# A post-LN attention and LoRA-FFN layer: the first two units' queries by seven products, the keys by tiles, gathers and sums in other slots, the end in another order

## The chip, the cores and the metric

The kernel runs on one NeuronCore of a Trainium2 chip. The metric is the time of one execution on the device in microseconds; a profiled execution gives the span from the first to the last instruction and the trace. The engines are TensorE (PE in the profile; its weight loads are PEld), VectorE (DVE), ScalarE (ACT), GpSimd (POOL) and SyncE (SP, which issues most of the DMAs here).

## The reference

The input x is 2 batches of 512 tokens of width 512, all in float32.

```python
q = x @ Wq + bq                  # 32 heads of 128
k = x @ Wk + bk ; v = x @ Wv + bv # 8 groups of 128
q, k = rope(q), rope(k)
scores = causal(q @ k.T / sqrt(128))     # each group serves 4 heads
ctx = softmax(scores) @ v
x = layernorm(x + ctx @ Wo + bo)

y = x @ W_base.T + b_base
z = x @ lora_A[active].T                 # 4 experts of rank 8
alpha = softmax(log(prior[active] + eps) + x @ router_W.T + router_b)
x = layernorm(x + y + sum_e alpha_e * 2 * z_e @ lora_B[e].T)
```

## The kernel before

**Units and slots.** A unit is a pair of a group (4 heads) and a batch; there are 16. After a setup written out by hand, the program is a sequence of slots T from -8 on; `slot(T)` issues what each engine does in that slot, and `put(T, f)` adds a step at its end. Each unit has 16 slots of attention: the slot's scores are one product of 128 rows (4 heads x 32 tokens) by up to 512 keys (`score`, L552), then VectorE's masked maximum (L560), ScalarE's exponential (L567), one slot apart each, with two banks of PSUM for scores. The order on every engine is the order of the program: it is a manual schedule, and each engine takes its instructions in that order.

**Products.** From unit 2 on, the queries of two heads and the output projection of two tiles are made by Strassen's scheme: seven products of half size in place of eight. `q_products(u, k, step)` (L440 by way of `product`) makes product `step` for the pair of heads k of unit u, in two half banks qx and qy. It needs sums of the weights (`w_sums`, four POOL instructions, L427 to L430), of which product 5 uses the first, 6 the second, 3 the third and 7 the fourth, and sums of x (`x_sums`, four VectorE instructions, L419). Products 1, 2 and 4 use weights as they are loaded. ScalarE copies a result out of qx (`q_copy`, L476) and VectorE adds qy (`q_sum`, L480). Rope takes three VectorE instructions a head (L374, L377, L381) and one POOL sum (L382). `wo_sums` (L637) are four VectorE sums of the output weights of a group, ahead of its products (`wo_products`).

**Setup before the change.** SP loads the four x tiles of the first batch, Wk of group 0, Wq of group 0, rope, Wq's second half, Wv, the second batch of x. POOL fills constants and two large zero tiles, issues six small DMAs of the expert indices (L217 to L220), an iota and two memsets (L227). TensorE turns the four x tiles (L281), multiplies the keys of unit 0 in four products of 512 columns (`k_mm`, L361), then unit 0's queries in sixteen plain products (`q_mm`, L361) with value tiles (`v_tile`, L344) and the second batch's transposes between. Unit 1's queries, sixteen plain products too, go one to each slot from -8 to 7. The prior's row (`prior_weights`) is three steps in slots -4 to -2; six gathers (`gather_experts`, indirect DMAs that POOL issues, L265) stand in slot -8; two steps of `lora_weights` in slots 12 and 16; sums of x of batch 0 in slots 0 to 3, of batch 1 in 12 to 15; `x + bo` (POOL, L899) in slots 2 to 9.

**The end.** From slot 237 on, the FFN of the first batch (f0) is mixed into the last units: W_base is loaded and turned (`transposed_base`), its copies on ScalarE. After the last slot, a hand-written order follows for the remaining tiles: fz (last of the first batch), fa (two), fb, fc. Each is `base` (x by W_base, L778), `logits` and `alphas` (VectorE, and an exponential on ScalarE), `low_rank` (a transpose, L814, and a copy, L815), `finish` (L819), `sum` (L829), statistics (L703), root (L711, ScalarE; inverse on VectorE) and `store`. `add` is `sum` and statistics.

Of the kernel before, what the change touches and what calls it, by code (L numbers as in the profile page):

```python
# [15 lines left out]
P = 128  # L16
# [13 lines left out]
def postln_layer_kernel(  # L30
# [117 lines left out]

    def load_k(g):
        wk_g = wts.tile([P, KC, D], F32, tag="wk_g", name=f"wk_{g}")  # L150
        nc.sync.dma_start(out=wk_g, in_=Wk[:, ts(g, D)].rearrange("(c p) n -> p c n", p=P))
        wqk["k", g] = wk_g
# [34 lines left out]
    nc.gpsimd.memset(eps_sb, LN_EPS)  # L187
    nc.gpsimd.memset(bmT, 0.0)
    for z in zt:
        nc.gpsimd.memset(z, 0.0)  # L190

    bqk = setup.tile([NBIAS, D], F32, name="bqk")
    nc.scalar.dma_start(out=bqk[:H, :], in_=bq.rearrange("(h d) -> h d", d=D))
    nc.scalar.dma_start(out=bqk[H : H + G, :], in_=bk.rearrange("(h d) -> h d", d=D))
    nc.scalar.dma_start(out=bqk[H + G :, :], in_=bv.rearrange("(h d) -> h d", d=D))
    for t in range(TPB):
        load_x(t, 1)
    load_k(0)
    load_q(0, 0)
# [69 lines left out]

    def gather_experts():  # L270
        gather(ar_act[:EAR, :], lora_A.rearrange("e r n -> (e r) n"), idx["a"])
        gather(ar_act[EAR : EAR + EA, :], router_W, idx["e"])
        for a in range(EA):
            gather(b_act[:, a, :], lora_B.rearrange("e (p j) r -> (e p) (j r)", j=BJ), idx["b"][:, a : a + 1])


    def transpose_token_tile(dst, src, pool, tag, copy):

        tp = pool.tile([P, KC, P], F32, tag=tag, name="tp")
        for c in range(KC):  # L280
            nc.tensor.transpose(tp[:, c, :], src[:, ts(c, P)], ident)  # L281
        copy(dst, tp)

    b_jar = setup.tile([P, BJ, EA, RK], F32, name="b_jar")

    def lora_weights(step):
        if step == 0:
            ta = ps_wo.tile([P, KC, EAR + EA], F32, tag="wx", name="ta")
            for c in range(KC):
                nc.tensor.matmul(  # L290
                    ta[:, c, :], lhsT=ar_act[:, ts(c, P)], rhs=ident[:, : EAR + EA], start=True, stop=True)
            nc.vector.tensor_copy(arT, ta)
            nc.vector.tensor_copy(b_jar, b_act.rearrange("p a (j r) -> p j a r", r=RK))
        else:

            tbm = ps_wo.tile([EAR, BJ, P], F32, tag="wx", name="tbm")
# [6 lines left out]
    def prior_weights(step):  # L303

        if step == 0:
            pr_eps = setup.tile([EA, 1], F32, name="pr_eps")
            nc.vector.tensor_scalar(pr_eps, pr_act, PRIOR_EPS, None, ALU.add)
            pr["lp"] = setup.tile([EA, 1], F32, name="lp")
            nc.scalar.activation(pr["lp"], pr_eps, AF.Ln)
        elif step == 1:  # L310
            lpb = setup.tile([EA, 1], F32, name="lpb")
            nc.vector.tensor_tensor(lpb, pr["lp"], rb_act, ALU.add)
            ones = setup.tile([EA, P], F32, name="ones")
            nc.vector.memset(ones, 1.0)
            nc.vector.tensor_scalar(lp_rep[:EA, :], ones, lpb, None, ALU.mult)
        else:
            pl = ps_wo.tile([P, EA], F32, tag="wx", name="pl")
            nc.tensor.matmul(pl, lhsT=lp_rep, rhs=ident[:, :EA], start=True, stop=True)
            nc.vector.tensor_copy(lp_bc, pl)
# [65 lines left out]
    def k_mm(u, c):  # L385
        g, b = unit(u)
        proj_mm(("k", u), ps_k, "k", wqk["k", g], slice(0, D), b, c)

    def k_of(u):
        if u not in kT:  # L390
            kT[u] = work.tile([P, UNIT, BLK], F32, tag="kT", name=f"kT_{u}", bufs=5)
        return kT[u]

    def k_rope(u, part):
        if part == 0:
            k_of(u)
        rope_step(("k", u), H + unit(u)[0], part, kT[u])

    def q_mm(u, r, c, pool, tag):

        g, b = unit(u)
        proj_mm(("q", u, r), pool, tag, wqk["q", set_of(u), r // 2], ts(r % 2, D), b, c)

# [10 lines left out]

    def x_sums(b, step):
# [3 lines left out]
        nc.vector.tensor_tensor(  # L419
            *((t1, b12, b11), (t2, b22, t1), (t3, b22, b12), (t4, b21, t2))[step], ALU.subtract)  # L420
# [541 lines left out]
    def slot(T):  # L962

        uq, step = divmod(T + 24, UNIT)
        kq, step = divmod(step, 8)
        now = B <= uq < NU
        if now and step != 7 and step != 4:
            q_products(uq, kq, {0: 2, 1: 6, 2: 5, 3: 7, 5: 4, 6: 3}[step])
        un, kn = (uq, 1) if kq == 0 else (uq + 1, 0)
        if B <= un < NU and step == 7:  # L970
            q_products(un, kn, 1)
        plain_q = T - T_BEGIN < UNIT and divmod(T - T_BEGIN, QB)
        if plain_q:
            r, c = plain_q
            q_mm(1, r, c, *q_banks[r])
        uk, l = divmod(T + UNIT, UNIT)
# [52 lines left out]
        kr, sr = divmod(sr, 8)  # L1029
        if B <= ur < NU and sr < 6:  # L1030
            q_rope(ur, 2 * kr + (sr < 3), sr % 3)
        r, part = divmod(T - T_BEGIN - QB, QB)
        if 0 <= r < R and part < 3:
            q_rope(1, r, part)
        k_slots = (4, 5, 6) if uk < PLAIN_K else (11, 13, 14) if uk < NU - 1 else (3, 5, 6)
# [9 lines left out]
    spare = ((ps_wo, "wx"), (ps_wo, "wy"), (ps_ctx, "ctx"), (ps_sc, "sc"))  # L1045
    q_banks = ((ps_q, "qx"), (ps_q, "qy"), (ps_q, "qx"), (ps_wo, "wy"))
# [6 lines left out]
    tb = ps_sc.tile([P, NBIAS], F32, tag="sc", name="tb")  # L1053
    nc.tensor.transpose(tb, bqk, ident[:NBIAS, :NBIAS])
    nc.vector.tensor_copy(bqkT, tb)
    for c in range(KC):
        k_mm(0, c)
    for part in range(3):
        k_rope(0, part)
    expert_rows()  # L1060

    for r in range(R):
        for c in range(KC):
            q_mm(0, r, c, *q_banks[r])
        for part in range(3):
            q_rope(0, r, part)
        if r == 2:
            for t in range(TPB, NT):
                transpose_token_tile(xT[:, :, ts(t, P)], x_sb[:, t, :], *spare[t % 2 + 2], nc.scalar.copy)
        elif r:  # L1070
            v_tile(0, r // 2, *spare[r // 2 * 2])
            v_out(0, r // 2)
    for t in range(2, TPB):
        v_tile(0, t, *spare[t % 2 * 2])
        v_out(0, t)

# [79 lines left out]
    f0[2].norm2.stats(2, f0[2].y)  # L1156
    f0[0].norm2.root(0, 3)
    for f in f0[:3]:
        f.store()
# [5 lines left out]
    fb.transpose(*CTX)  # L1165
    fz.logits()
    fz.alphas()
    for r in range(R):
# [105 lines left out]
```

## Time and profile before

| What | Value |
|---|---|
| runs | 822.33, 823.33, 825.24 us; median 823.33 |
| the profiled execution | 822.99 us |
| its span | 821.2 us |
| TensorE | busy 810.6 us, granted clock 0.999 |
| VectorE, ScalarE, POOL | busy 603.7, 379.2, 320.9 us |
| DMA | 116.00 MB, mean 141 GB/s |
| first product of the keys; of unit 0's queries | at 8.38; at 11.92 us |
| first product of a slot's scores | at 45.62 us |
| last product | starts at 815.2 us |

Times in rows of the trace are from the start of the span. A row of the timeline gives start, duration, engine, line, operation, the tensors written and read, and the shape; "x8" is eight merged records. A float32 matmul shows as two records. Busy time of an engine is not by itself time that can be saved: what matters is what ends the wait of the engine that sets the end.

### The profile page before, as it was taken

The numbers are of one execution on the slowest core, as the hardware profiler recorded it, in microseconds if no ns is written. First come the engines' busy times: TensorE is split into PE (matmuls) and PEld (weight loads), VectorE is DVE, ScalarE is ACT, GpSimd is POOL, SyncE is SP. The second block draws the span as 40 slices with busy tenths as digits, with TensorE's granted clock in tenths as the row PEclk, the third lists the DMA queues.
The fourth block names the chain that finished last, engine by engine and source line by source line (L and its number), as shares of the span: only waits on it lengthen the run. The fifth ranks groups of instructions, "written<-read, shape, count | busy, mean of one in ns | idle before, by whom it ended". The sixth has DMA issues, their size and how long they took to land.

```text
span 821.2 us, 11196 instructions
## 1 busy us (share of the span) xinstructions
PE 810.6 (99%) x3385; PEld 598.5 (73%) x3385; DVE 603.7 (74%) x1972; ACT 379.2 (46%) x1058; POOL 320.9 (39%) x377
## 2 busy tenths in 40 slices
PE   8999999999999999999999999999999999999996
PEld 5567777777777778777777878777777878655565
DVE  4367877677878876787868777787888689974455
ACT  1236453453545554444545444444545454663244
POOL 6464343512543545321453245343464333420033
PEclk9999999999999999999999999999999999999999
DMA  9015636445474637354454627355453726674211
GB/s 306 22 39 148 213 77 174 134 118 163 103 208 107 201 91 218 90 141 156 135 150 126 190 66 224 97 154 180 134 148 96 225 65 183 187 257 142 77 39 65
DMA packets 84415, 116.00 MB, mean 141 GB/s; under 512 B 6525, under 2 KB 64237, under 8 KB 82306
## 3 DMA queue, kind: packets, MB, share of 16 engines
q1 hardware_dynamic: 83682, 114.98, 48.7%
q8 instruction: 27, 0.44, 0.2%
q14 instruction: 34, 0.28, 0.1%
q0 software_dynamic: 448, 0.14, 0.1%
q10 hardware_dynamic: 224, 0.16, 0.1%
HBM read 71.21 MB, written 44.04 MB: 140 GB/s over the span
## 4 chain that ended last, share of the span: by engine, by line
PE 94%; DVE 3%; ACT 1%; DMA 1%; issue 0%; POOL 0%; SPq 0%; DVEq 0%; POOLq 0%
PE pc L608 16%; PE sc L552 14%; PE qx L440 12%; PE wx L440 11%; PE qy L440 9%; PE wy L440 9%; PE pp L361 5%; PE kx L440 4%; PE vx L518 4%; PE py L778 3%; PE po L684 3%; PE pv L344 3%; PE tp L281 1%; PE py L819 1%; DMA x_sb<-_attn_hidden_states_dram 1%; DVE st L703 0%
## 5 line engine op out<-in xcount | busy, mean ns | idle before, releaser
L560 DVE CUSTOM_DVE_ANT_0 sc<-sc,maskw 128x288 f32<-128x288 f32 (+15 forms) x256 | 114.2, 446 | 139.6 <-PE sc L552 138.1
L567 ACT ACTIVATE p<-sc,nmax 128x288 f32<-128x288 f32 (+15 forms) x256 | 124.3, 485 | 200.5 <-DVE nmax L560 179.0
L608 PE MATMUL pc<-pT,v 128*128 128x512 f32 x320 | 165.4, 599 | 0.0
L552 PE MATMUL sc<-kT,qT 128*128 128x160 f32 (+15 forms) x512 | 161.8, 398 | 1.0 <-ACT p L567 1.0
L382 POOL TENSOR_TENSOR qT<-q,t 128x512 f32<-128x512 f32 x56 | 76.5, 1365 | 178.8 <-DVE q L381 176.0
L575 ACT ACTIVATE p<-p,den 128x288 f32<-128x288 f32 (+15 forms) x256 | 133.2, 521 | 0.0
L552 PEld LDWEIGHTS sc<-kT,qT 128*128 128x128 f32 x512 | 96.1, 190 | 23.9 <-issue 9.8
L615 ACT ACTIVATE ctxT<-pc,bqkT 128x512 f32<-128x512 f32 x64 | 44.0, 687 | 118.0 <-PE pc L608 118.0
L427 POOL TENSOR_TENSOR cs<-ctxT 128x256 f32<-128x256 f32 x28 | 22.5, 802 | 157.7 <-PE wy L440 94.5
L583 DVE STREAM_TRANSPOSE zt<-p 128x128 f32<-128x128 f32 (+2 forms) x192 | 81.6, 425 | 0.0
L608 PEld LDWEIGHTS pc<-pT,v 128*128 128x128 f32 x320 | 57.1, 190 | 18.7 <-issue 5.7
L440 PE MATMUL qx<-xs,wq 128*128 128x256 f32 x224 | 58.0, 381 | 0.0
L476 ACT COPY q<-qx 128x256 f32<-128x256 f32 x112 | 41.4, 370 | 35.2 <-PE qx L440 35.1
L440 PEld LDWEIGHTS qx<-xs,wq 128*128 128x128 f32 x224 | 41.4, 190 | 22.2 <-issue 18.4
L440 PE MATMUL wx<-wo,ctxT 128*128 128x256 f32 x224 | 57.6, 379 | 0.0
L585 DVE STREAM_TRANSPOSE zt<-p 128x32 f32<-128x32 f32 (+3 forms) x256 | 57.5, 225 | 0.0
L567 ACT ACTIVATION_READ_ACCUMULATOR p<-sc,nmax 128x1 f32 x256 | 49.8, 195 | 0.0
L440 PEld LDWEIGHTS wx<-wo,ctxT 128*128 128x128 f32 x224 | 42.5, 190 | 7.7 <-issue 1.4
L670 DVE TENSOR_TENSOR x_sb<-wx,x_sb 128x256 f32<-128x256 f32 x112 | 47.0, 420 | 0.0
L374 DVE SCALAR_TENSOR_TENSOR t<-q,bqkT,rope_sb 64x512 f32<-64x512 f32 x56 | 45.6, 815 | 1.5
L377 DVE SCALAR_TENSOR_TENSOR t<-q,bqkT,rope_sb 64x512 f32<-64x512 f32 x56 | 42.7, 762 | 1.3
L571 DVE RECIPROCAL den<-den 128x1 f32<-128x1 f32 x256 | 39.3, 153 | 1.3 <-ACT p L567 1.2
(233 smaller groups left out, 1482.1 us busy)
## 6 DMA issues: line engine op xcount, KB each, us to landing
db<-zt SPq DMA_DIRECT2D x64, 256.0 KB, 4.2
pT<-db SPq DMA_DIRECT2D x16, 1024.0 KB, 4.8
db<-zt SPq DMA_DIRECT2D x64, 192.0 KB, 3.2
pT<-db SPq DMA_DIRECT2D x16, 768.0 KB, 4.5
wq<-in_L_attn_Wq_dram SPq DMA_DIRECT2D x20, 512.0 KB, 5.1
wo<-in_L_attn_Wo_dram SPq DMA_DIRECT2D x10, 1024.0 KB
db<-zt SPq DMA_DIRECT2D x64, 128.0 KB, 2.3
pT<-db SPq DMA_DIRECT2D x16, 512.0 KB, 4.1
```

The source lines that it names most:

```text
L374: nc.vector.scalar_tensor_tensor(t2[lo, :], q[hi, :], b_ap[hi, :], rope_sb[hi, 1, :], ALU.add, ALU.mult)
L382: nc.gpsimd.tensor_tensor(dst, t1[:, :].rearrange("p (n s) -> p n s", s=BLK), t2[:, :].rearrange("p (n s) -> p n s", s=BLK), ALU.add)
L440: nc.tensor.matmul(ps, lhsT=wt[:, c, :], rhs=xt[:, c, :], start=start and c == 0, stop=c == CH - 1, skip_group_check=True)
L552: nc.tensor.matmul(sc[s][:, :w], lhsT=qT[u][:, i * QB + n].rearrange("p r s -> p (r s)"), rhs=kT[u][:].rearrange("p n s -> p (n s)")[:, :w ...
L560: nc.vector.tensor_tensor_reduce(sc[s][:, :w], sc[s][:, :w], maskw[:, S - w :], -SCALE, -MASKED, ALU.add, ALU.min, nmax[s])
L567: nc.scalar.activation(ptile[s][:, :w], sc[s][:, :w], AF.Exp, bias=nmax[s], scale=-1.0, accum_out=rden[s])
L575: nc.scalar.activation(ptile[s][:, :w], ptile[s][:, :w], AF.Copy, scale=rden[s])
L583: nc.vector.transpose(z[:, :, last - i : last, n, :].rearrange("p q j s -> p j q s"), ptile[s][:, : i * P])
L585: nc.vector.transpose(z[:, : n + 1, last, n, :], ptile[s][:, i * P : w])
L608: nc.tensor.matmul(psc[p], lhsT=v_sb[g // VG, b][:, j, ts(g % VG, D)], rhs=pT[p][:, :, ts(j, P)], start=(j == 0), stop=(j == i))
L615: nc.scalar.activation(ctxT[p], psc[p], AF.Identity, bias=bqkT[:, col : col + 1])
L670: nc.vector.tensor_tensor(into, pw[k, bank], into, ALU.add)
```

## The change

It does the following.

- **Queries of units 0 and 1** are made by the seven products too: unit 0's in the setup, unit 1's in slots -8 to 7 by the same rule as later units. So `w_sums(0, k)` and `x_sums(0, ...)` stand at the start of the setup, and `x_sums(1, ...)` go to POOL in the middle of it. `q_mm` is gone.
- **Keys of unit 0** are multiplied tile by tile (128 tokens), each two tiles behind the transposes; their weights are loaded first on ScalarE's queue instead of SP's. The last x tile is turned into two half banks, copied by two engines.
- **Value tiles** of the first batch, and one of the second, are in the setup; the other three in slots -4, 4 and 6.
- **Gathers** go one to a slot: -5, -4, -3, 7, 8, 9. **The prior's row** is summed on POOL in slot 5, and its product stands in slot 12. **The experts' transposes** use the keys' bank, in slots 13 and 14.
- `x + bo` goes from slots 2 to 9 to slots 12 to 19, the first `wo_sums` from slots 21 to 24 to 16 to 19, and group 1's `w_sums` four slots later.
- **The end**: two of the transposes of W_base one slot earlier; fz's logits and alphas ahead of the stores; the second fa tile's statistics and root behind fb's low-rank copy.

```diff
-    def load_k(g):
+    def load_k(g, queue=nc.sync):
...
+    load_k(0, nc.scalar)
     bqk = setup.tile([NBIAS, D], F32, name="bqk")
...
-    load_k(0)
...
-            nc.vector.tensor_tensor(lpb, pr["lp"], rb_act, ALU.add)
+            nc.gpsimd.tensor_tensor(lpb, pr["lp"], rb_act, ALU.add)
...
+    def k_tile(u, t, c):
+
+        g, b = unit(u)
+        key = "k", u
+        if t == c == 0:
+            psq[key] = ps_k.tile([P, S], F32, tag="k", name="pp")
+            in_psum.add(key)
+        nc.tensor.matmul(
+            psq[key][:, ts(t, P)], lhsT=wqk["k", g][:, c, :], rhs=xT[:, c, ts(b * TPB + t, P)],
+            start=(t == c == 0), stop=(c == KC - 1), skip_group_check=True)
...
-    put(T_BEGIN, gather_experts)
-    for n, gg, t in [(2 * t - 1, 0, TPB + t) for t in range(TPB)] + [(2 * t + 11, 1, t) for t in range(TPB)]:
+    for k in range(2 + EA):
+        put((-5, -4, -3, 7, 8, 9)[k], lambda k=k: gather_experts(k))
+    for n, gg, t in [(n, 0, TPB + 1 + k) for k, n in enumerate((-4, 4, 6))] + [(2 * t + 11, 1, t) for t in range(TPB)]:
...
-    for n in range(TPB):
-        put(n, lambda n=n: x_sums(0, n))
-        put(n + 12, lambda n=n: x_sums(1, n))
-    for k in range(3):
-        put(-4 + k, lambda k=k: prior_weights(k))
-        if k < 2:
-            put(12 + 4 * k, lambda k=k: lora_weights(k))
+    for k in range(2):
+        put((5, 12)[k], lambda k=k: prior_weights(k + 1))
+        put(13 + k, lambda k=k: lora_weights(k))
...
-        put(2 + t, lambda t=t: nc.gpsimd.tensor_tensor(x_sb[:, t, :], x_sb[:, t, :], bo_bc, ALU.add))
+        put(12 + t, lambda t=t: nc.gpsimd.tensor_tensor(x_sb[:, t, :], x_sb[:, t, :], bo_bc, ALU.add))
...
-            put(q_from(set_units(n)[0], k) - 9, lambda n=n, k=k: w_sums(n, k))
+            put(q_from(set_units(n)[0], k) - (5 if n == 1 else 9), lambda n=n, k=k: w_sums(n, k))
...
-        at = {NSETS - 4: (-16, -15, -15, -13), NSETS - 3: (-11, -9, -6, -5)}.get(n, (0, 1, 1, 3))
+        at = {0: (-5, -4, -3, -2), NSETS - 4: (-16, -15, -15, -13), NSETS - 3: (-11, -9, -6, -5)}.get(n, (0, 1, 1, 3))
...
-        now = B <= uq < NU
+        now = 0 < uq < NU
...
     for t in range(TPB):
-        transpose_token_tile(xT[:, :, ts(t, P)], x_sb[:, t, :], *spare[t], copies[t % 2])
...
+        x_to = xT[:, :, ts(t, P)], x_sb[:, t, :]
+        if t > 1:
+            for c in range(KC):
+                k_tile(0, t - 2, c)
+        if t < TPB - 1:
+            transpose_token_tile(*x_to, *spare[t], copies[t % 2])
+        else:
+            for n, bank in enumerate((spare[t], (ps_q, "qx"))):
+                transpose_token_tile(*x_to, *bank, copies[n], range(2 * n, 2 * n + 2))
...
+    for t in range(TPB - 2, TPB):
         for c in range(KC):
-            q_mm(0, r, c, *q_banks[r])
...
+            k_tile(0, t, c)
+    for n in range(4):
+        x_sums(0, n)
+    for k in range(2):
+        w_sums(0, k)
...
+    for k in range(2):
+        for step in (1, 2, 6, 5, 7):
+            q_products(0, k, step)
+            if step == 1:
+                q_copy(0, k, "p1")
+            elif step == 2:
+                q_sum(0, k, "p1")
+                if k:
+                    q_rope(0, 0, 2)
+                    for part in range(3):
+                        k_rope(0, part)
+                    for n in range(3):
+                        x_sums(1, n, nc.gpsimd)
...
+        q_sum(0, k, "u3")
+        if k == 0:
+            expert_rows()
+        v_first(2 * k)
+        q_products(0, k, 4)
+        q_copy(0, k, "c21")
+        if k:
+            prior_weights(0)
+            q_rope(0, 3, 0)
+        q_products(0, k, 3)
+        q_sum(0, k, "u2")
+        v_first(2 * k + 1)
...
+                    xT[:, :, ts(t, P)], x_sb[:, t, :], *spare[(2, 3, 0, 3)[t - TPB]], nc.scalar.copy)
...
+            x_sums(1, 3, nc.gpsimd)
+            for part in range(3):
+                put(T_BEGIN + part, lambda part=part: q_rope(0, 2, part))
...
+    v_first(TPB)
+    q_products(1, 0, 1)
...
-        put(T_PROJ + (4, 6, 8, 10)[c], lambda c=c: transposed_base(c))
+        put(T_PROJ + (3, 6, 8, 9)[c], lambda c=c: transposed_base(c))
...
     f0[0].norm2.root(0, 3)
+    fz.logits()
+    fz.alphas()
...
-    fz.logits()
-    fz.alphas()
...
-    fa[1].add()
-    fa[1].norm2.sqrt(1, 2)
+    fa[1].sum()
...
     fb.low_rank()
-    fa[1].norm2.invert(1, 2)
+    fa[1].norm2.stats(1, fa[1].y)
+    fa[1].norm2.root(1, 2)
```

More of the change, by code (lines that the diff above doesn't have):

```diff
@@ L147, in postln_layer_kernel @@
     wvs = {}
-    def load_k(g):
+    def load_k(g, queue=nc.sync):
         wk_g = wts.tile([P, KC, D], F32, tag="wk_g", name=f"wk_{g}")
-        nc.sync.dma_start(out=wk_g, in_=Wk[:, ts(g, D)].rearrange("(c p) n -> p c n", p=P))
+        queue.dma_start(out=wk_g, in_=Wk[:, ts(g, D)].rearrange("(c p) n -> p c n", p=P))
         wqk["k", g] = wk_g
@@ L268, in gather, with gather_experts, transpose_token_tile @@
         )
[L270 to L273, printed above, removed]
-            gather(b_act[:, a, :], lora_B.rearrange("e (p j) r -> (e p) (j r)", j=BJ), idx["b"][:, a : a + 1])
[L277 to L282, printed above, removed]
+    def gather_experts(step):
+        if step == 0:
+            gather(ar_act[:EAR, :], lora_A.rearrange("e r n -> (e r) n"), idx["a"])
+        elif step == 1:
+            gather(ar_act[EAR : EAR + EA, :], router_W, idx["e"])
+        else:
+            a = step - 2
+            gather(b_act[:, a, :], lora_B.rearrange("e (p j) r -> (e p) (j r)", j=BJ), idx["b"][:, a : a + 1])
+    def transpose_token_tile(dst, src, pool, tag, copy, chunks=range(KC)):
+        tp = pool.tile([P, len(chunks), P], F32, tag=tag, name="tp")
+        for n, c in enumerate(chunks):
+            nc.tensor.transpose(tp[:, n, :], src[:, ts(c, P)], ident)
+        copy(dst[:, chunks[0] : chunks[-1] + 1, :], tp)
     b_jar = setup.tile([P, BJ, EA, RK], F32, name="b_jar")
@@ L287, in lora_weights @@
         if step == 0:
-            ta = ps_wo.tile([P, KC, EAR + EA], F32, tag="wx", name="ta")
+            ta = ps_k.tile([P, KC, EAR + EA], F32, tag="k", name="ta")
             for c in range(KC):
@@ L294, in lora_weights @@
         else:
-            tbm = ps_wo.tile([EAR, BJ, P], F32, tag="wx", name="tbm")
+            tbm = ps_k.tile([EAR, BJ, P], F32, tag="k", name="tbm")
             for j in range(BJ):
@@ L311, in prior_weights @@
             lpb = setup.tile([EA, 1], F32, name="lpb")
-            nc.vector.tensor_tensor(lpb, pr["lp"], rb_act, ALU.add)
+            nc.gpsimd.tensor_tensor(lpb, pr["lp"], rb_act, ALU.add)
             ones = setup.tile([EA, P], F32, name="ones")
-            nc.vector.memset(ones, 1.0)
-            nc.vector.tensor_scalar(lp_rep[:EA, :], ones, lpb, None, ALU.mult)
+            nc.gpsimd.memset(ones, 1.0)
+            nc.gpsimd.tensor_scalar(lp_rep[:EA, :], ones, lpb, None, ALU.mult)
         else:
-            pl = ps_wo.tile([P, EA], F32, tag="wx", name="pl")
+            pl = ps_wo.tile([P, EA], F32, tag="wy", name="pl")
             nc.tensor.matmul(pl, lhsT=lp_rep, rhs=ident[:, :EA], start=True, stop=True)
@@ L397, in k_rope @@
         rope_step(("k", u), H + unit(u)[0], part, kT[u])
-    def q_mm(u, r, c, pool, tag):
-        g, b = unit(u)
-        proj_mm(("q", u, r), pool, tag, wqk["q", set_of(u), r // 2], ts(r % 2, D), b, c)
     CH = KC // 2
@@ L413, in postln_layer_kernel, with x_sums @@
     halves = {}
-    def x_sums(b, step):
+    def x_sums(b, step, engine=nc.vector):
         b11, b12, b21, b22 = (
@@ L418, in x_sums @@
         t1, t2, t3, t4 = (xs[:, b, k] for k in range(4))
-        nc.vector.tensor_tensor(
+        engine.tensor_tensor(
             *((t1, b12, b11), (t2, b22, t1), (t3, b22, b12), (t4, b21, t2))[step], ALU.subtract)
@@ L969, in slot @@
         un, kn = (uq, 1) if kq == 0 else (uq + 1, 0)
-        if B <= un < NU and step == 7:
+        if un < NU and step == 7:
             q_products(un, kn, 1)
[L972 to L975, printed above, removed]
         uk, l = divmod(T + UNIT, UNIT)
@@ L1029, in slot @@
         kr, sr = divmod(sr, 8)
-        if B <= ur < NU and sr < 6:
+        if 0 < ur < NU and sr < 6:
             q_rope(ur, 2 * kr + (sr < 3), sr % 3)
-        r, part = divmod(T - T_BEGIN - QB, QB)
-        if 0 <= r < R and part < 3:
-            q_rope(1, r, part)
         k_slots = (4, 5, 6) if uk < PLAIN_K else (11, 13, 14) if uk < NU - 1 else (3, 5, 6)
@@ L1045, in postln_layer_kernel @@
     spare = ((ps_wo, "wx"), (ps_wo, "wy"), (ps_ctx, "ctx"), (ps_sc, "sc"))
-    q_banks = ((ps_q, "qx"), (ps_q, "qy"), (ps_q, "qx"), (ps_wo, "wy"))
     idle = ps_sc.tile([P, 2 * P], F32, tag="sc", name="idle")
@@ L1051, in postln_layer_kernel @@
     for t in range(TPB):
-        transpose_token_tile(xT[:, :, ts(t, P)], x_sb[:, t, :], *spare[t], copies[t % 2])
[L1053 to L1062, printed above, removed]
-        for c in range(KC):
-            q_mm(0, r, c, *q_banks[r])
-        for part in range(3):
-            q_rope(0, r, part)
-        if r == 2:
-            for t in range(TPB, NT):
[L1069 to L1072, printed above, removed]
@@ L1073, in postln_layer_kernel @@
-    for t in range(2, TPB):
-        v_tile(0, t, *spare[t % 2 * 2])
-        v_out(0, t)
+        x_to = xT[:, :, ts(t, P)], x_sb[:, t, :]
[4 more added lines that the diff above has]
+            transpose_token_tile(*x_to, *spare[t], copies[t % 2])
+        else:
+            for n, bank in enumerate((spare[t], (ps_q, "qx"))):
+                transpose_token_tile(*x_to, *bank, copies[n], range(2 * n, 2 * n + 2))
+        if t == 2:
+            tb = ps_sc.tile([P, NBIAS], F32, tag="sc", name="tb")
+            nc.tensor.transpose(tb, bqk, ident[:NBIAS, :NBIAS])
+            nc.vector.tensor_copy(bqkT, tb)
@@ new lines, in postln_layer_kernel, with v_first @@
+    for t in range(TPB - 2, TPB):
+        for c in range(KC):
+            k_tile(0, t, c)
[3 more added lines that the diff above has]
+        w_sums(0, k)
+    def v_first(t):
+        v_tile(0, t, *spare[t % 2])
+        v_out(0, t)
+    for k in range(2):
[11 more added lines that the diff above has]
+                        x_sums(1, n, nc.gpsimd)
+            elif step == 6:
+                q_copy(0, k, "u2")
+            elif step == 7:
+                q_copy(0, k, "u3")
+        q_sum(0, k, "u3")
[10 more added lines that the diff above has]
+        v_first(2 * k + 1)
+        if k == 0:
+            for t in range(TPB, NT):
+                transpose_token_tile(
+                    xT[:, :, ts(t, P)], x_sb[:, t, :], *spare[(2, 3, 0, 3)[t - TPB]], nc.scalar.copy)
+        for part in range(k, 3):
+            q_rope(0, 2 * k + 1, part)
+        if k:
+            x_sums(1, 3, nc.gpsimd)
+            for part in range(3):
+                put(T_BEGIN + part, lambda part=part: q_rope(0, 2, part))
+        else:
+            for part in range(2):
+                q_rope(0, 0, part)
```

## The prediction

> **What bounds the kernel now.** I read the page's busy shares and slices first, then the chain that ended last, then what TensorE waited for, then the timeline of the stretches that the change edits.
>
> ```profile
> span 821.2 us, 11196 instructions
> PE 810.6 (99%) x3385; PEld 598.5 (73%) x3385; DVE 603.7 (74%) x1972; ACT 379.2 (46%) x1058; POOL 320.9 (39%) x377
> ...
> PE   8999999999999999999999999999999999999996
> ...
> PEclk9999999999999999999999999999999999999999
> ...
> PE 94%; DVE 3%; ACT 1%; DMA 1%; issue 0%; POOL 0%; SPq 0%; DVEq 0%; POOLq 0%
> ```
>
> TensorE is busy in every slice but the first and the last, at a full clock, and makes 94% of the chain. A busy PE need not be a dense one, so I take the chain in order of time (start, us, what) and divide:
>
> ```profile
> 2.12 4.88 DMA x_sb<-_attn_hidden_states_dram
> ...
> 20.67 3.43 PE pp L361 x8
> ...
> 88.87 0.86 PE qy L440 x4
> ...
> 280.36 0.89 PE vx L518 x8
> ```
>
> Each record is one of the two passes of a float32 product. A pass of 512 columns takes 3.43/8 = 0.429 us, of 256 columns 0.86/4 = 0.215, of 128 columns 0.89/8 = 0.111: time goes with columns, so the weight loads are hidden and the queue is dense. What TensorE waited for is therefore short (us in total, times, longest):
>
> ```profile
> PE sc L552 <- ACT p L567: 1.0, 1, 1.0
> PE py L819 <- DVE zT L815: 0.5, 1, 0.5
> PE pp L361 <- ACT xT L282: 0.5, 1, 0.5
> ...
> PE tz L814 <- DVE zs L805: 0.2, 1, 0.2
> ```
>
> So a change gains by taking columns from TensorE, by starting it earlier than 8.4 us (where the keys' products begin), or by removing one of these waits; all else is cover, and costs nothing until it makes TensorE wait. The front decides, so here is its timeline (start, us):
>
> ```profile
> 6.23 0.81 POOL L217 DMA_DIRECT2D act_e<-in_L_ffn_active_dram  x1
> ...
> 10.27 0.23 POOL L227 MEMSET lp_rep<- 128x128 f32 x1
> ...
> 11.92 7.03 PE L361 MATMUL pp<-xT,wq 128*128 128x512 f32 x16
> ...
> 43.22 0.81 DVE L419 TENSOR_TENSOR xs<-xT 128x512 f32<-128x512 f32 x1
> 43.55 1.05 POOL L428 TENSOR_TENSOR ws<-ws,wq 128x256 f32<-128x256 f32 x1
> 44.69 0.73 POOL L429 TENSOR_TENSOR ws<-wq,ws 128x256 f32<-128x256 f32 x1
> ```
>
> The queries start at 11.92; POOL is done with its own setup at 10.50; a sum of weights takes 0.73 on POOL, and 1.05 beside a sum of x on VectorE.
>
> **1. Seven products.** Removed: 2 units x 4 heads x 4 chunks x 2 passes = 64 passes of 512 columns, 64 x 0.429 = 27.5 us. Added: 2 units x 2 pairs x 7 products x 2 chunks x 2 passes = 112 passes of 256, 112 x 0.215 = 24.1. All on the path: **-3.4 us**. What the products need besides: sixteen copies on ScalarE (0.37 each, the L476 rows) and twelve VectorE sums (0.42, L480). From 8.4 to 62.6 us ScalarE is busy 13 of 54 us and VectorE 29.5, and VectorE gives up 3 us of sums of x there, so nothing.
>
> **2. Keys by tiles, and the sums that gate the queries.** Before, the last x tile is transposed at 7.05, its copy ends at 8.33, and the keys' 3.54 us follow: queries at 11.92. Now tiles 0 to 2 are multiplied while later tiles arrive, and only tile 3 (8 passes, 0.9 us) is left behind the last copy, which two engines share. The keys' load goes to ScalarE's queue and meets the x tiles: 0.25 MB at the 250 to 340 GB/s of the DMA row is 0.7 to 1.0 us later for x. I get the last key product at 9.3 to 10.4. The keys' price is a place where the Trainium skill speaks against the change. The row says 0.111 us for a pass of 128 columns: 32 passes make 3.55, against 3.43 for the whole tile, so +0.1. "TensorE: Matmul & The Clock Gate", section Back-to-back issue gap, says that in a stream with weight loads a matmul of 128 columns is spaced 81 ns where its columns alone give 56: scaled, 0.155 x 32 = 5.0, or +1.5 us. The L518 row is this very shape with a load before each product; I take 0.1.
>
> But product 6 needs POOL's second sum of weights, and POOL comes to it at 10.50. Two sums at 0.73 with gaps of 0.08 end at 12.1; beside VectorE's four sums of x (0.65 to 0.97 each, from the last copy on) at the 1.05 of the row, 12.7. "SBUF — State Buffer", section Who interferes with whom, is harsher: a VectorE instruction with two SBUF inputs and a GpSimd one that reads SBUF exclude each other for a whole instruction, so up to two sums of x (0.65 each) in the way: 13.4. The row lost 0.32, not 0.65; I take 12.6. Products 1 and 2 (1.7 us) are done by then, so the queries have in effect started at 12.6 - 1.7 = 10.9: **-1.0 us**; the bounds are -1.5 (12.1) and -0.2 (13.4).
>
> **3. The rest of the setup.** The second x tiles now take four banks instead of two; TensorE's only gap inside the setup, 0.4 us at 25.2 waiting for ScalarE to free a bank, goes: **-0.4**. Value tiles move, and cost the same. The four sums of x of the second batch go to POOL, behind the keys' rope add; at 1.27 us (L899, 128x512) to 1.72 (beside VectorE) the second ends near 31 to 32, while unit 1's product 6 comes near 35: 3 us of cover. Behind them in POOL's queue stand the rope adds of heads 2 and 3 (1.27 each) and, in slots -5 to -3, three gathers (1.0 + 0.3 each); the first score waits for the rope adds alone, done near 38, against slot 0 near 42. Nothing.
>
> **4. Slots 5 to 19.** Prior's row on POOL: three small operations, hidden, and its matmul stays. Gathers in slots 7 to 9: the last is issued near 61, lands 5.1 to 5.4 us later (as the two gathers at 16 and 17 us did), near 67; VectorE's copy of it in slot 13 comes near 71. Nothing, with 4 us of cover; if late, every masked maximum queues behind that copy. Experts' transposes keep their passes, in a bank free between the keys of units 1 and 2. The doubtful edit is that the first sums of Wo move from slots 21-24 to 16-19, and the bias adds on POOL from 2-9 to 12-19. There they meet: such a sum takes 0.69 alone and 1.76 beside POOL. VectorE is busy 16.4 of 20 us in 80 to 100; it loses the sums of x of slots 12 to 15 (3 us) and gets 2.8 to 7. TensorE today loses 0.3 near 102 behind a Wo sum of 1.76. Bounds: that 0.3 saved, or up to 4 lost; nearest is the row of slots 21 to 24, one collision in four, so I take a loss of 0.5 and the 0.3 saved: **+0.2**.
>
> **5. The end.** A transpose of W_base moves one slot ahead: its copy (0.59) leaves ScalarE's queue just before the 1.0 us wait of a score for an exponential (721 us). ScalarE was idle 0.5 us a slot earlier, so about half goes: **-0.5** (bounds 0 and -1.1). Expert weights of the last first-batch tile earlier: its exponential stood behind ctx, three copies and a table load, until 791.4; TensorE's next product starts 0.4 late (at 792.98): **-0.4**. Statistics after the low-rank copy: takes a 0.5 wait from TensorE at 812.7, but there VectorE's own chain (sum, statistics, root, next statistics) sets the end, and it now idles for the root's 0.36: **+0.2**.
>
> Sum: -3.4 - 1.0 - 0.4 + 0.2 - 0.5 - 0.4 + 0.2 = **-5.3 us**. The profiled execution took 822.99 us (span 821.2 and 1.8 around it), 0.34 under the median of 823.33; both move alike: 817.7 and **818.0**.
>
> **Rivals.** (A) POOL becomes the bound of the front and the end gives nothing: product 6 at 13.4, no gain at 721 or in the tail. Then -3.4 - 0.2 - 0.4 + 0.5 = -3.5: 819.8. For it: POOL enters at 10.5 whatever the keys do, so keys by tiles don't do what they are for. Against: one collision, not two, per row. 22%. (B) Better: 12.1 at the front, no collision at slots 16 to 19, all of the wait at 721: -0.5, -0.5, -0.6 and -0.2 (the end's loss) on top of -5.3, so -7.1: 816.2. 10%. (C) Slower: VectorE becomes the bound in slots 12 to 19. If each of the eight bias adds holds up one VectorE operation by the 1.05 us of the worst row (a sum of x at 1.73 against 0.69), that is 8.4 us, and 2.8 for the Wo sums, against some 3.6 us free and 1.5 that two score banks absorb: TensorE waits 6.1, and the time is 824. It ends slower from a wait of 5.3 on. Against: in slots 2 to 9 the same adds met the sums of x, and one of the eight took 1.72 us, the rest 1.27. 13% for a wait above 3 us, of which half is over 5.
>
> **From cases to numbers.** This kernel's measurement can tell about 0.3% (2.5 us) from no change. The likeliest case, 55%, spans 816.8 to 819.4; A 22% at 819.8, B 10% at 816.2, C 13% at 821 to 826. The range 815.5 to 821.6 leaves out little of B and most of C. Faster by over 0.3% (under 820.9): 0.81; within: 0.11; slower: 0.08.
>
> **What would show it.** Right: L440 with 112 passes more and L361's queries gone; the first query product near 10 and the first product with a summed weight near 12.6, waiting for POOL L428; slot 8's products 4.5 to 5 us earlier than 62.55; no new TensorE wait above 0.5 from 13 to 90 us; the 0.97 of the score at 721 halved. Wrong: waits of scores for VectorE near slots 16 to 20, product 6 of unit 1 waiting for POOL's sums of x, VectorE idle at the copy of the gathered rows, or x tiles landing over 1 us later.

## The result, and the profile after

The changed kernel takes **817.38 us** in the median of 6 runs (816.90 to 818.26), the kernel before 823.19 in 6 runs on the same chip (822.33 to 825.24): ratio 0.9925, 95% interval 0.991 to 0.9939. The forecast was 818.0. The profiled execution took 816.90 us with a span of 815.1, 6.06 us under the span before. First the page: busy shares, slices, clock, and the chain's shares by engine.

```profile
span 815.1 us, 11389 instructions
PE 807.0 (99%) x3457; PEld 609.7 (75%) x3457; DVE 609.8 (75%) x1978; ACT 384.9 (47%) x1074; POOL 338.6 (42%) x392
...
PE   9999999999999999999999999999999999999996
...
PEclk9999999999999999999999999999999999999999
...
PE 96%; POOL 1%; DVE 1%; ACT 1%; issue 0%; POOLq 0%
```

TensorE is as full as before, with 3.6 us less of work. What is new is POOL's 1% in the chain. What TensorE waited for over the whole span (us in total, times, longest) has shrunk to three entries; the waits of before for a low-rank copy (0.5), for an x copy (0.5) and at the last transposes (0.2) are gone, and that for an exponential is 0.3 in place of 1.0:

```profile
PE idle L1049 <- DVE maskw L176: 1.2, 1, 1.2
PE tp L285 <- DMA x_sb<-_attn_hidden_states_dram: 0.4, 1, 0.4
PE sc L562 <- ACT p L577: 0.3, 1, 0.3
```

Where the 6.06 us came from is read by setting the two timelines side by side at one landmark per slot, the start of its first score product (us earlier than before; the last two rows are a transpose of the end and the end of the span):

| Landmark | earlier by | what lies behind the step |
|---|---|---|
| slot 8 | 4.86 | front, seven products of units 0 and 1, gaps of the setup |
| slot 24 to slot 236 | 4.77 | Wo sums, bias adds, gathers: 0.09 lost |
| slot 243 | 5.42 | a transpose of W_base one slot earlier: +0.65 |
| fz's transpose | 5.80 | its logits and alphas earlier: +0.38 |
| end of the span | 6.06 | the tail: +0.26 |

The front, from the chain of the changed kernel in order of time (start, us, what). Before, this chain began with the DMA of x; now it runs through POOL's queue from its first constant to the second sum of weights, and only there passes to TensorE:

```profile
3.16 3.13 POOL zt L191 x2
6.28 0.74 POOL act_e L218
...
9.86 0.48 POOL ar_act L228
...
10.55 1.15 POOL ws L437
...
11.78 1.07 POOL ws L438
...
12.88 1.13 PE qx L450 x4
```

### The profile page after: what moved, and what is told of

It is laid out like the page before. It is cut to its first block, busy times and chain, and to the rows that moved or that the text cites. A ratio compares the mean times of both kernels' runs of the same rounds, so it can differ in the third digit from the quotient of the medians.

```text
span 815.1 us, 11389 instructions
## 1 busy us (share of the span) xinstructions
PE 807.0 (99%) x3457; PEld 609.7 (75%) x3457; DVE 609.8 (75%) x1978; ACT 384.9 (47%) x1074; POOL 338.6 (42%) x392
## 4 chain that ended last, share of the span: by engine, by line
PE 96%; POOL 1%; DVE 1%; ACT 1%; issue 0%; POOLq 0%
PE pc L618 17%; PE sc L562 15%; PE qx L450 14%; PE wx L450 12%; PE qy L450 10%; PE wy L450 9%; PE kx L450 4%; PE vx L528 4%; PE po L694 3%; PE py L788 3%; PE pv L348 3%; PE pp L365 1%; PE tp L285 1%; PE py L829 1%; POOL zt L191 0%; POOL act_er L220 0%
## 5 line engine op out<-in xcount | busy, mean ns | idle before, releaser
L386 POOL TENSOR_TENSOR qT<-q,t 128x512 f32<-128x512 f32 x64 | 88.0, 1376 | 176.1 <-DVE q L385 165.0
L486 ACT COPY q<-qx 128x256 f32<-128x256 f32 x128 | 47.4, 370 | 51.4 <-PE qx L450 49.8
L450 PE MATMUL qx<-xs,wq 128*128 128x256 f32 x256 | 66.3, 381 | 0.0
L450 PEld LDWEIGHTS qx<-xs,wq 128*128 128x128 f32 x256 | 47.3, 190 | 23.2 <-issue 18.4
L378 DVE SCALAR_TENSOR_TENSOR t<-q,bqkT,rope_sb 64x512 f32<-64x512 f32 x64 | 52.3, 818 | 3.5 <-ACT q L486 1.7
L381 DVE SCALAR_TENSOR_TENSOR t<-q,bqkT,rope_sb 64x512 f32<-64x512 f32 x64 | 50.3, 786 | 1.5
L385 DVE SCALAR_TENSOR_TENSOR q<-q,bqkT,rope_sb 128x512 f32<-128x512 f32 x64 | 48.1, 751 | 0.1
```

The lines of the kernel that those rows point to most:

```text
L378: nc.vector.scalar_tensor_tensor(t2[lo, :], q[hi, :], b_ap[hi, :], rope_sb[hi, 1, :], ALU.add, ALU.mult)
L381: nc.vector.scalar_tensor_tensor(t2[hi, :], q[lo, :], b_ap[lo, :], rope_sb[lo, 1, :], ALU.add, ALU.mult)
L385: nc.vector.scalar_tensor_tensor(t1, q, b_ap, rope_sb[:, 0, :], ALU.add, ALU.mult)
L386: nc.gpsimd.tensor_tensor(dst, t1[:, :].rearrange("p (n s) -> p n s", s=BLK), t2[:, :].rearrange("p (n s) -> p n s", s=BLK), ALU.add)
L450: nc.tensor.matmul(ps, lhsT=wt[:, c, :], rhs=xt[:, c, :], start=start and c == 0, stop=c == CH - 1, skip_group_check=True)
```

## The experiments

"Later" and "earlier" are against the changed kernel's median of 817.38; ratios are to the kernel before, on the same chip. The first four kernels shared one chip, the next four another, the last four a third, and the kernel before gave medians of 822.32, 822.56 and 822.82 there, against 823.19 beside the changed kernel. So a difference below about 0.9 us between two medians of this list is not told apart from what chips and runs do by themselves, and where one is that small only the rows can speak. The changed kernel itself was run once more in the third group (the last entry), as a measure for the others.

**Keys whole again** (keys_whole).

```diff
-        if t > 1:
-            for c in range(KC):
-                k_tile(0, t - 2, c)
...
-    for t in range(TPB - 2, TPB):
-        for c in range(KC):
-            k_tile(0, t, c)
+    for c in range(KC):
+        k_mm(0, c)
```

> The changed kernel with unit 0's keys in four products of 512 columns again, behind the last x tile; all else as changed. My theory (TensorE's work sets the front once POOL's second sum of weights is there, at 12.8 us): the keys end near 12.0, product 6 of unit 0 starts near 13.7 instead of 12.9 and no longer waits for POOL; every later product and the end come 0.8 us later, 817.7 us in the profiled execution against 816.9. Rival (POOL gates the front alone, tiles gain nothing): product 6 stays at 12.9, 816.9. Second rival (the tiles' gain is whole): 1.1 us and more.

Measured: 817.84 (817.71 to 821.63, 5 runs), ratio 0.9942 (0.9925 to 0.9959). The median is 0.5 later, which is too little to tell from no change. The profiled run is the slowest, 821.63, and its TensorE rows (start, us) show what was slow in it:

```profile
5.66 1.97 PE L285 MATMUL tp<-ident,x_sb 128*128 128x128 f32 x8 [0.35 <-DMA x_sb<-_attn_hidden_states_dram]
...
7.83 1.12 PE L285 MATMUL tp<-ident,x_sb 128*128 128x128 f32 x4
9.08 5.61 PE L365 MATMUL pp<-xT,wk 128*128 128x512 f32 x8
```

Eight passes of 512 columns take 5.61 us, 0.70 each, where the kernel before needed 3.70; four transposes take 1.12 instead of 0.60. The passes ran at half speed until about 13.2, although the clock row of these windows reads 1.00. By slot 0 this run is 3.2 us behind the changed kernel's, much of it from this, and it loses 1.4 more in two later waits for probabilities on their way through DRAM (0.58 at 269.6, 0.31 at 698.9, and what follows them). The other four runs, 817.71 to 818.29, have no trace. So what the tiles are worth is not shown: the expected 0.8 is neither met nor excluded. Nor is it shown that their absence made TensorE slow. It was busy for 3.59 of the 4 us from 5 to 9 here, for 3.64 in the changed kernel and for only 2.38 in the kernel before, where the same passes ran at full speed.

**Early key weights on SP's queue, behind x** (wk_on_sp).

```diff
-    load_k(0, nc.scalar)
...
         load_x(t, 1)
+    load_k(0)
     load_q(0, 0)
```

> The changed kernel with group 0's key weights loaded on SP's queue behind the four x tiles, as before the change. My theory (the keys by tiles need the weights early, and with them in line behind x the first tile's product waits until near 7.2 us and all tiles follow): last key product near 11.7, product 6 near 13.5, the end 0.6 us later, 817.5. Rival (the two queues share the same DMA engines, so the place of the load doesn't matter): no difference, 816.9, or a little earlier because x is not held up.

Measured: 820.64 (818.65 to 821.63, 9 runs), ratio 0.9969 (0.9955 to 0.9983): 3.3 later, five times what was expected. It begins with one wait:

```profile
7.85 1.13 PE L400 MATMUL pp<-xT,wk 128*128 128x128 f32 x8 [2.05 <-DMA wk<-in_L_attn_Wk_dram]
```

From about 9 to 12.5 TensorE then runs at half speed (four transposes take 0.81 and 0.99 instead of 0.60, and the granted clock from 9.0 to 13.2 is 0.59), and at 17.91 it waits 0.85 more for VectorE. Slot 8 is 0.79 ahead of the kernel before instead of 4.86: 4.1 lost, twice the wait that began it.

**POOL later, and POOL earlier** (pool_late, pool_early). The first puts two more fills of a tile (0.55 each) ahead of the sums of weights; the second moves the two fills of the zero tiles (3.13) behind them.

```diff
     for n in range(4):
         x_sums(0, n)
+    for n in range(2):
+        nc.gpsimd.memset(ar_act, 0.0)
     for k in range(2):
```

```diff
-    for z in zt:
-        nc.gpsimd.memset(z, 0.0)
...
         w_sums(0, k)
+    for z in zt:
+        nc.gpsimd.memset(z, 0.0)
```

> The changed kernel with two more POOL memsets of 512 columns (0.55 us each) ahead of the first sums of weights. My theory (product 6 waits for POOL's second sum): product 6 and everything behind it 1.1 us later, 818.0 in the profiled execution. Rival (the wait at product 6 is for VectorE's sums of x, or there is slack elsewhere in the setup that takes it up): less than 0.3 us.

> The changed kernel with the two large zero tiles' memsets (3.1 us of POOL) behind the sums of weights instead of ahead of the index DMAs. My theory: POOL reaches the sums as soon as the query weights have landed, product 6 follows product 2 at 12.6 to 12.7 without a wait, and the end is 0.3 to 0.4 us earlier, 816.5. Rival (VectorE's sums of x then end the wait): no gain. Second rival (the zero tiles, or the index DMAs, are now late): slower.

Measured: later 817.74 (817.56 to 817.86), ratio 0.9942 (0.9925 to 0.9959); earlier 817.96 (817.80 to 818.17), 0.9945 (0.9928 to 0.9962). Neither time differs enough to be told from the changed kernel's; the rows decide. With POOL 1.1 late, product 6 comes at 13.55 instead of 12.88, and now its row names the wait, so the gate is POOL:

```profile
13.55 1.13 PE L450 MATMUL qx<-xs,ws 128*128 128x256 f32 x4 [0.97 <-POOL ws L438]
```

Only 0.67 of the 1.1 arrive, since the sums of x are done by then: of the three sums of weights that were stretched to 1.05 to 1.14, two now take 0.73, and the two sums of x that had met them take 0.68 instead of 1.22. With POOL early nothing is won either. These are its VectorE rows (this kernel's line numbers are two lower):

```profile
10.22 1.03 DVE L427 TENSOR_TENSOR xs<-xT,xs 128x512 f32<-128x512 f32 x1
11.17 1.21 DVE L427 TENSOR_TENSOR xs<-xT 128x512 f32<-128x512 f32 x1
12.30 1.21 DVE L427 TENSOR_TENSOR xs<-xT,xs 128x512 f32<-128x512 f32 x1
13.43 0.41 DVE L488 TENSOR_TENSOR q<-qy,q 128x256 f32<-128x256 f32 x1
```

Product 6 starts at 12.42 without a wait, but three sums of x now collide, `q_sum` comes at 13.43, and product 5 waits for it until 13.90. POOL and VectorE bound the front together: freeing one hands the wait to the other.

**Unit 1 by plain products** (unit1_plain). Its odd heads are then multiplied by the summed weights that stand in place of the loaded ones; shapes and number of products are those of the plain scheme.

```diff
-        now = 0 < uq < NU
+        now = B <= uq < NU
...
+        plain_q = T - T_BEGIN < UNIT and divmod(T - T_BEGIN, QB)
+        if plain_q:
+            r, c = plain_q
+            proj_mm(("q", 1, r), *q_banks[r], wqk["q", 0, r // 2], ts(r % 2, D), 1, c)
```

> The changed kernel with unit 1's queries by sixteen plain products in slots -8 to 7 again; unit 0 keeps its seven. The weights that unit 0's sums overwrite are used as they stand, so part of unit 1's odd heads is another sum than the reference's; time only is read. My theory (TensorE's columns are the whole gain of this part): 32 passes of 512 columns for 56 of 256 cost 13.7 - 12.1 = 1.7 us, all at the end: 818.6. Rival (the copies and sums that the seven products need cost back part of it on ScalarE and VectorE): under 1 us.

Measured: 819.96 (819.48 to 820.74, 5 runs), ratio 0.9965 (0.9951 to 0.9979). From slot 0 to slot 8 the changed kernel gains 3.42 us on the kernel before, this one 1.72, which is a value tile that both have moved out of these slots: one unit's seven products are worth the other 1.70. The whole run is 2.6 later, 0.9 more than the 1.7 expected. The profiled run, 3.8 later, shows where more can go: 0.80 lies before slot 0, where the edit leaves TensorE's columns the same, and 0.55 and 0.72 at two products (697.4 and 722.35) that wait for their probabilities' DMA.

**The end alone, in the kernel before** (before_end).

```diff
-        put(T_PROJ + (4, 6, 8, 10)[c], lambda c=c: transposed_base(c))
+        put(T_PROJ + (3, 6, 8, 9)[c], lambda c=c: transposed_base(c))
...
+    fz.logits()
+    fz.alphas()
...
-    fa[1].add()
-    fa[1].norm2.sqrt(1, 2)
+    fa[1].sum()
...
-    fa[1].norm2.invert(1, 2)
+    fa[1].norm2.stats(1, fa[1].y)
+    fa[1].norm2.root(1, 2)
```

> The kernel before with the edits of the end alone: W_base's transposes a slot earlier, fz's logits and alphas ahead of the stores, the second fa tile's statistics behind fb's low-rank copy. My theory as the changed kernel's trace leaves it: 0.65 us from the score's wait at 721 us, 0.4 from the product at 793, 0.25 behind, together 1.3 us: 821.7 in the profiled execution against 822.99. Rival (the recorded step: the last of the three costs 0.2): 822.2. Second rival (the end gains only because the front has shifted it against the DMAs): 823.

Measured: 821.78 (821.58 to 822.63, 10 runs), ratio 0.999 (0.9981 to 1.0). That is 0.8 less than the kernel before on this chip, where 1.3 was expected. In its trace the wait at 721 gives 0.61, of which the next product of probabilities, which waits for its DMA, takes 0.47 back (it starts 0.37 later after its score, at 723.45); fz's transpose gives 0.39, the tail 0.25. So the gain at 721 can be lost again to the next wait. It is not the slots that decide: with the change's own slots, the same place takes back 0.72 in the trace of unit 1 by plain products and 0.15 and 0.17 with POOL later and earlier, and nothing in the two traces of the changed kernel. What makes this DMA land late in some executions stays open.

**Bias adds back in slots 2 to 9** (bias_back), **Wo sums back in slots 21 to 24** (wo_back).

```diff
-        put(12 + t, lambda t=t: nc.gpsimd.tensor_tensor(x_sb[:, t, :], x_sb[:, t, :], bo_bc, ALU.add))
+        put(2 + t, lambda t=t: nc.gpsimd.tensor_tensor(x_sb[:, t, :], x_sb[:, t, :], bo_bc, ALU.add))
```

```diff
-        at = {0: (-5, -4, -3, -2), NSETS - 4: (-16, -15, -15, -13), NSETS - 3: (-11, -9, -6, -5)}.get(n, (0, 1, 1, 3))
+        at = {NSETS - 4: (-16, -15, -15, -13), NSETS - 3: (-11, -9, -6, -5)}.get(n, (0, 1, 1, 3))
```

> The changed kernel with x + bo on POOL in slots 2 to 9 again, all else as changed. My theory (these adds meet VectorE's operations with two SBUF inputs in slots 12 to 19, and TensorE lost only 0.24 us near 92 by it): that wait goes, but POOL's queue in slots 2 to 9 holds the gathers too, so between 0.2 us earlier and 0.5 later: 816.7 to 817.4. Rival (the move is what keeps POOL free for the weights' sums and gathers): more than 1 us later, with VectorE waiting at the copy of the gathered rows.

> The changed kernel with the first four sums of Wo on VectorE in slots 21 to 24 again. My theory: the wait of 0.24 us near 92 goes and the one of 0.33 near 97 (102 before) comes back: 0.1 us later, 817.0. Rival (moving them is what the rest of the middle needs): 0.5 us later or more. Second rival (collisions on POOL's port are the cost in slots 16 to 19): 0.3 earlier.

Measured: bias_back 824.86 (822.42 to 825.36, 10 runs), ratio 1.0024 (1.0014 to 1.0033), **7.5 later**: moving eight cheap adds back loses more than the whole change gains. My theory fell. wo_back 818.02 (817.31 to 818.22), ratio 0.994 (0.9923 to 0.9957), 0.6 later, too little to tell from no change; between slots 12 and 24 its profiled run loses 0.27 more than the changed kernel's, and 0.97 in the front, which the edit doesn't touch.

In bias_back slot 8 is still 4.49 ahead of the kernel before; slot 11 is 2.4 behind it. TensorE's waits from 45 to 75 us (there are none in the changed kernel):

```profile
PE qy L450 <- DVE q L490: 1.7, 1, 1.7
PE sc L562 <- ACT p L577: 1.4, 1, 1.4
PE qx L450 <- ACT q L486: 0.8, 1, 0.8
```

The last of the three comes first in time, at 60.34, and it is POOL's doing: ScalarE's copy may overwrite its buffer only when POOL's rope add at 58.63, which stands behind a bias add, has read it.

```profile
59.92 0.37 ACT L486 COPY q<-qx 128x256 f32<-128x256 f32 x1 [2.58 <-POOL kT L386]
```

The other two, at 62.84 and 65.31, come from VectorE's queue running late, and that from one row of its timeline first of all. A rotation that takes 0.75 us takes 4.73:

```profile
56.93 4.73 DVE L378 SCALAR_TENSOR_TENSOR t<-q,bqkT,rope_sb 64x512 f32<-64x512 f32 x1
...
62.52 1.92 DVE L381 SCALAR_TENSOR_TENSOR t<-q,bqkT,rope_sb 64x512 f32<-64x512 f32 x1
```

Beside it POOL's rows, three adds without a gap from 57.40 to 61.11:

```profile
57.40 1.26 POOL L906 TENSOR_TENSOR x_sb<-x_sb,bo_bc 128x512 f32<-128x512 f32 x1
58.63 1.25 POOL L386 TENSOR_TENSOR kT<-t,t 128x512 f32<-128x512 f32 x1
59.85 1.26 POOL L906 TENSOR_TENSOR x_sb<-x_sb,bo_bc 128x512 f32<-128x512 f32 x1
```

The rotation began 0.47 us before the first of these adds and ended 0.55 after the last: these times fit one that stood still between. Note the operand: `t<-q`. With seven products the queries are put together in SBUF, so the rotation has two SBUF inputs, q and the rope table. With plain products it reads `t<-pp`, from PSUM. "SBUF — State Buffer", section Terms, says that VectorE and GpSimd arbitrate for a shared port pair which is held for a whole instruction while the loser blocks, and its section on the two sides of SBUF names a VectorE operation with two SBUF inputs as a case. These rows agree, and show more: VectorE did not get in between back-to-back adds. A count over six traces (the kernel before and after, bias_back, unit1_plain, and the two kernels below) says the same of all rotations. Of those that read PSUM, 63 ran beside a sum or product on POOL, and every one took 0.71 to 0.76 us. Of those that read SBUF, 947 ran without one and took 0.70 to 0.75; 349 ran beside one, and 202 of these took over 0.8, of which 4.73 is the longest. A second loss follows in TensorE (busy us of PE, PEld, DVE, ACT and POOL in each stretch, then the granted clock):

```profile
60.00:66.00 6.00, 2.63 (x8) 1.58 (x9) 5.93 (x14) 2.63 (x9) 5.65 (x5) 0.84 0.58 171
66.00:72.00 6.00, 6.00 (x16) 4.34 (x15) 5.92 (x14) 2.67 (x8) 5.14 (x5) 0.59 0.18 39
```

Having been idle for 3.4 of 6 us, TensorE is granted 0.59 of its clock for the next 6. Of the 7.5 us, the three waits are 3.8; most of the rest falls in this stretch. That it comes again from run to run is seen in the clock over the whole span: it is 0.993 to 0.995 in nine of the ten runs, where the changed kernel has 0.998 or 0.999, and 0.998 in the fastest, which took 822.42, 5.0 later. "TensorE: Matmul & The Clock Gate", Part 1, describes a gate that watches how busy the array has been; the row agrees.

Two more kernels test this reading of one trace.

**Bias adds in slots 2 to 9, unit 1 by plain products** (bias_plain): the edits of bias_back and unit1_plain together.

> The change with the x + bo adds back in slots 2 to 9, as in the run that came out at 824.9, and with unit 1's odd heads by summed weights, so that its rotation reads q from PSUM and not from SBUF. Lock theory: VectorE's rotation with two SBUF inputs is held for as long as POOL's adds follow each other without a gap (4.73 us in that run); with q in PSUM it has one SBUF input, nothing is held, and the bias adds cost under 1 us against the run with unit 1 plain alone (819.96): 820 to 821, no rotation over 2 us. Rival, POOL's queue: the rotation's own add on POOL waits behind bias adds and gathers, whatever VectorE reads: 824 to 827, with the same waits at 60 to 65 us.

Measured: 819.41 (818.67 to 820.00, 4 runs), ratio 0.9957 (0.9942 to 0.9972). That is not later than unit 1 plain alone (819.96). POOL's adds lie even closer, four in a row from 57.40 to 62.34:

```profile
57.40 1.26 POOL L906 TENSOR_TENSOR x_sb<-x_sb,bo_bc 128x512 f32<-128x512 f32 x1
58.62 1.25 POOL L386 TENSOR_TENSOR qT<-t,t 128x512 f32<-128x512 f32 x1
59.85 1.26 POOL L386 TENSOR_TENSOR kT<-t,t 128x512 f32<-128x512 f32 x1
61.08 1.26 POOL L906 TENSOR_TENSOR x_sb<-x_sb,bo_bc 128x512 f32<-128x512 f32 x1
```

and VectorE's rotation beside the last of them takes its ordinary time:

```profile
61.30 0.75 DVE L378 SCALAR_TENSOR_TENSOR t<-pp,bqkT,rope_sb 64x512 f32<-64x512 f32 x1
```

From slot 8 to slot 24 this trace gains 0.11 us on the kernel before, where bias_back's loses 7.23. POOL's queue is much the same, the rotation's source differs, and the 7.5 us are gone. So the rival (POOL's queue) does not explain the loss. It keeps a small part of it: ScalarE's copy waits for POOL until 59.91 here too, but unit 1's plain products give TensorE more to do meanwhile, and it waits for nothing, where bias_back's TensorE waited 0.77. The edit also takes unit 1's own copies and sums from ScalarE and VectorE; that VectorE has fewer of these is a second difference, which no run here separates from the rotation's source. The counted rotations speak for the source.

**Bias adds in slots 12 to 19, in the kernel before** (before_bias).

```diff
-        put(2 + t, lambda t=t: nc.gpsimd.tensor_tensor(x_sb[:, t, :], x_sb[:, t, :], bo_bc, ALU.add))
+        put(12 + t, lambda t=t: nc.gpsimd.tensor_tensor(x_sb[:, t, :], x_sb[:, t, :], bo_bc, ALU.add))
```

> The kernel before with one edit: the x + bo adds at slots 12 to 19 in place of 2 to 9. Lock theory: there units 0 and 1 read q from PSUM, so nothing is held in slots 2 to 9 before, and the move alone is worth nothing: ratio 0.9995 to 1.001 (822.2 to 824). Rival, early adds always cost: a gain of 2 us or more (821 or less). Second rival, from the record of the forecast: at slots 12 to 19 the adds run into the Wo sums and cost 0.5 us or more there.

Measured: 824.26 (823.77 to 825.95, 11 runs), ratio 1.0019 (1.001 to 1.0028): the move alone costs 1.4 us. Nothing changes up to slot 22; the loss lies in slots 23 and 24, where TensorE waits 1.03 us at 103.29 for VectorE's sum of a query and 0.23 for a Wo sum. POOL's sums of ctx, behind the bias adds, come at 92.9 to 96.7 instead of 88.6 to 92.0, and the Wo sums on VectorE take 1.38 and 1.75. So the second rival was right: by itself the move is a loss, and it pays only beside unit 1's seven products.

**Two more edits in the end** (best2).

```diff
-        put(T_PROJ + (3, 6, 8, 9)[c], lambda c=c: transposed_base(c))
+        put(T_PROJ + (10, 6, 8, 9)[c], lambda c=c: transposed_base(c))
...
-    fa[0].norm2.sqrt(0, 1)
-    fc.low_rank(*CTX)
-    fa[0].norm2.invert(0, 1)
-    fa[0].store()
     fb.logits()
+    fc.low_rank(*CTX)
     fb.alphas()
     fa[1].finish()
+    fa[0].norm2.sqrt(0, 1)
     fa[1].sum()
+    fa[0].norm2.invert(0, 1)
+    fa[0].store()
```

> The change with two more edits. W_base's first tile is transposed at step 10 in place of 3 of its stretch, so that its copy on ScalarE doesn't lie ahead of the softmax whose probabilities TensorE waits 0.35 us for at 715.9; and the last but one tile's logits and alphas come ahead of the root of the tile before it, so that the table load of 1.28 us lies behind its exponential. If both are on the path: 0.3 to 0.6 off the wait and 0.4 to 0.8 off the tail, 816.1 to 816.7. If the wait moves to the next softmax and the tail is bound by another chain: 817.4, no change.

**The change once more** (after_again), no edit.

> The changed kernel as it stands, once more, beside the one with two more edits and on the same chip: 817.4, between 816.9 and 818.3. It tells how far the front moves from run to run with no edit at all: the first key product lay between 5.8 and 6.4 us in the runs so far with the same front, and the first query product between 10.7 and 11.6.

Measured: best2 817.88 (817.16 to 818.26, 5 runs), ratio 0.9939 (0.9926 to 0.9953); after_again 817.54 (816.92 to 817.80, 5 runs), 0.9936 (0.9922 to 0.9949). The two edits don't make it faster. In best2 TensorE's pauses ahead of the score at 716 are 0.56 us in all, where the changed kernel has 0.61, so the transpose that was moved away had filled time in which TensorE would have waited anyway; a product of probabilities at 719.15 costs 0.39 besides. From slot 236 to slot 255 it gains 0.09 on the kernel before, the changed kernel 0.65. The tail gives 0.07 more. The second run of the change has its first queries at 11.16 behind a wait of 0.34 for their weights, and product 6 at 13.25 instead of 12.88, as POOL's first sum waits 0.65 for the same weights; its slot 8 gains 3.97 instead of 4.86. With no edit at all, the front moves by 0.9 us from one profiled run to the next, so no single trace can judge an edit of the front below that.

## Why the prediction was right, step by step

- **Seven products, -3.4: right.** Unit 1 alone measures 1.70, and twice that is 3.4; unit 0's were not taken out alone.
- **Front, -1.0: the mechanism was right, its size -0.8 in the first trace and -0.4 in the second.** Product 6 came at 12.88 and 13.25, not 12.6; less the 1.75 of products 1 and 2, the queries in effect began at 11.1 and 11.5, against 11.92. The undersized term is the collisions: in the first trace two sums of weights were stretched (1.15 and 1.07), where I had counted one. In the second, the first sum waited for the query weights' DMA, a term that my sum did not have. A second error hid behind it: the keys should have ended at 9.3 to 10.4, with "only tile 3" left behind the last copy; the first query product came at 10.89. TensorE is dense from 5.36 on, with twelve transposes (0.44 a tile) and 32 passes (3.55), so the earlier tiles' products were not free either. POOL's gate covered that. Of the two prices for a pass of 128 columns the row was right: sixteen passes from 9.11 to 10.89, 0.111 each.
- **Setup, -0.4: right**, sixteen transposes run in 1.75 us with no gap. Of slot 8's 4.86 us, 3.4 + 0.8 + 0.4 leave 0.26, about the pause of before ahead of the prior's product (0.44 between 40.94 and 41.38, with 0.1 of work in it), which I had not counted. In the second trace the same terms make 4.2 for a slot 8 of 3.97, so they are good to about 0.3.
- **Slots 5 to 19, +0.2: measured +0.09, by luck of the sum rather than by its working.** Wo sums and bias adds met (one at 83.72 took 1.67) and TensorE lost 0.24 near 92. But I had priced only where the bias adds went. What they left was worth 7.5 us: my sum took the eight adds of slots 2 to 9 at 1.27 us as harmless because they were harmless before, and did not ask what the new rotation would read. Rival C was near it, with VectorE operations held up by the bias adds, but at the wrong slots; that its price for the adds, 8.4 us, is near 7.5 is luck, since it is one short hold for each add, where the run shows one long hold, a wait for POOL and a lowered clock.
- **721, -0.5: right**, 0.65 in both traces of the change, though other kernels with the same edit gave up to 0.72 back at the next product. **fz, -0.4: right**, 0.38.
- **Tail, +0.2: wrong sign**, -0.26. The root is on the chain as I said (0.30 at 806.74), but with its inverse and the statistics of a half (0.79 together) it stands where the chain before had the low-rank products (0.71). From the last but one sum to the last, 2.56 us became 2.51, and that last sum takes 0.67 where its two halves took 0.87.

By these sizes the first trace adds up: 4.77 + 0.65 + 0.38 + 0.26 = 6.06. The forecast's 5.3 is nearer to the medians (5.8 and 5.3 under the kernel before on their chips) than this trace is.

## What to carry to other kernels

When an edit changes where an operand lives, PSUM or SBUF, look again at every POOL instruction that runs beside its readers: a cheap add may turn into a stop of several microseconds for VectorE. Price what a moved step leaves behind as well as where it lands, and test such moves together and alone: here the same move gained 7.5 us beside the seven products and cost 1.4 without them. When a wait is named for one engine, find what is next late before freeing it.

## What the runs showed of the hardware that was not expected

- Three POOL adds without a gap held one VectorE rotation with two SBUF inputs for 4.0 us beyond its own 0.75, while 63 rotations that read PSUM lost nothing beside POOL. A hold is not always so long: at 83.72 in the changed kernel a Wo sum beside two such adds took 1.67 instead of 0.69 and ended 0.55 after the first of them, and the second took 1.71 instead of 1.28, so there VectorE came in between. What decides between the two was not tried.
- TensorE lost half its speed for a few microseconds after it had idled: 3.4 of 6 us in bias_back, then a clock of 0.59 over the next 6; a single wait of 2.05 us in wk_on_sp, then 0.59 from 9.0 to 13.2. In the front of keys_whole it ran at half speed up to about 13.2 without any wait above 0.35 us since its first transpose, and the row reads 1.00. There the passes' own lengths and the row disagree, and why it was slow stays open.
